# Layer 2 of a two-layer interaction network in fp32: seven half-width products over tile pairs instead of eight, with sums of products on GpSimd

## The chip, the cores and the metric

The kernel runs on one core of a Trainium2 chip. The metric is the device time of one execution in microseconds (us). A core has a matrix engine (TensorE, PE in the profile; its weight loads have a row of their own, PEld), VectorE (DVE), ScalarE (ACT), GpSimd (POOL) and SyncE (SP, which here only starts transfers). SBUF is the on-chip memory of 128 partitions, PSUM the accumulator memory that PE writes, in banks of 128 x 512 fp32 numbers; DVE and ACT read and write both.

## The reference

`x` has 4096 rows, 32 fields, 16 embedding positions; row and position together are 65,536 sites. All is fp32.

```python
def _batchnorm(h, gamma, beta):                       # over rows and positions
    mean = jnp.mean(h, axis=(0, 2), keepdims=True)
    var = jnp.var(h, axis=(0, 2), keepdims=True)
    return (h - mean) * jax.lax.rsqrt(var + EPS) * gamma[None, :, None] + beta[None, :, None]

def _cin_layer(out, x, W, b, gamma, beta):
    r, _, e = x.shape
    h = jnp.einsum('rne,rfe->rnfe', out, x).reshape(r, -1, e)
    h = jnp.einsum('rce,oc->roe', h, W) + b[None, :, None]
    return _batchnorm(h, gamma, beta)

h1 = _cin_layer(x, x, W1, b1, g1, beta1)              # 128 channels from 32 x 32 products
out, direct1 = (h1[:, :64], h1[:, 64:])
direct2 = _cin_layer(out, x, W2, b2, g2, beta2)       # 128 channels from 64 x 32 products
return jnp.concatenate([direct1, direct2], axis=1).sum(axis=-1)
```

## The kernel before

The sites lie along the free axis, in 128 tiles of 512. Tiles 2c and 2c+1 form one of 64 chunk pairs (the index `c` of the code; a pair below): one tile from each half of the sites.

**Layer 1** makes, for each tile, products of fields with fields (`z`, DVE, L208), multiplies them with the weights (PE, L218 and L220), and reads the sum out of PSUM (ACT, L176, L179, L189). DVE takes batch-norm statistics (L79) and sums over positions (L192). The 64 kept channels of a pair go to DRAM as `hs[c]`. Each tile has two loads, `a` and `b`, of 512 KB; each has three buffers, and SP issues them in the order of the tiles. The accumulators of four tiles are opened at once by four matmuls that use 32 rows of the array each (L218); `psum1` has eight banks.

**Between the layers** the batch-norm of layer 1 becomes a scale and a shift. Four small matmuls spread them to the partitions of layer 2, and a few matmuls without use (`running`) keep PE busy.

**Layer 2** has 2048 products per site, 16 blocks of 128: four groups `i` of 16 kept channels, and in each four chunks `k` of eight fields. For each tile and group ACT applies scale and shift to the group's channels into a PSUM tile (`factor`, L296), DVE multiplies it by four chunks of fields at once (`z`, 128 x 2048, L306), and PE accumulates four full-width matmuls (L311). A tile thus has 16 matmuls in one bank; ACT reads it out (L316), DVE takes statistics (L79) and position sums (L318). Per pair SP loads two `b` of 1024 KB and four `a` of 512 KB.

Each engine works strictly in the order in which it got its instructions. A product tile has three buffers (`zpool`), a factor tile three, an accumulator four banks. At the end the batch-norm of layer 2 is applied to the 128 x 2048 position sums of each half (L328), which are then stored.

Of the kernel before, what the change touches and what calls it, by code (L numbers as in the profile page):

```python
# [35 lines left out]
RT = T // EMB  # L36
KEEP = 64
EPS = 1e-5
WRAP = 48
GROUP = 8  # L40
SG = 16


@with_exitstack
def tile_cin(ctx: ExitStack, tc: tile.TileContext, xa, xb, xr, w1, w1m, w2, bn, out):
    nc = tc.nc

    const = ctx.enter_context(tc.tile_pool(name="const", bufs=1))
    dram = ctx.enter_context(tc.tile_pool(name="dram", bufs=1, space=bass.MemoryType.DRAM))
# [4 lines left out]
    bpool = ctx.enter_context(tc.tile_pool(name="bpool", bufs=3))  # L54
    apool = ctx.enter_context(tc.tile_pool(name="apool", bufs=8))
# [11 lines left out]
    class Stats:  # L67


        def __init__(self, n):  # L70
            self.n = n
            self.groups = const.tile([P, NT // SG, 3], FP, tag=f"groups{n}", name=f"groups{n}")
            nc.vector.memset(self.groups, 1.0)

        def add(self, t, h, bias=None):

            if t % SG == 0:
                self.stats = spool.tile([P, SG, 6], FP, tag="stats", name=f"stats{self.n}")
            nc.vector.bn_stats(self.stats[:, t % SG, :], h)  # L79
            if bias is not None:  # L80
                means = self.stats[:, t % SG, 1:5:3]
                nc.vector.tensor_scalar(means, means, bias, None, ALU.add)
            if t % SG == SG - 1:
                nc.vector.bn_aggr(self.groups[:, t // SG, 1:3], self.stats.rearrange("p a b -> p (a b)"))  # L84

        def scale_shift(self, gamma, beta):
# [13 lines left out]
            ss = const.tile([P, 3], FP, tag=f"ss{self.n}", name=f"ss{self.n}")  # L100
# [5 lines left out]

    select = const.tile([KEEP, 4, 16, 8], FP, tag="select", name="select")
    nc.gpsimd.memset(select, 1.0)  # L110
    nc.gpsimd.affine_select(
        out=select,
# [6 lines left out]
    )  # L119

    hs = [dram.tile([KEEP, 2 * T], FP, tag=f"h{c}", name=f"h{c}") for c in range(NC)]
    d1 = sums.tile([P, ROWS // 2], FP, tag="sum", name="d1")
    stats1 = Stats(1)

    with ExitStack() as one:
        wpool = one.enter_context(tc.tile_pool(name="wpool", bufs=1))
        lpool = one.enter_context(tc.tile_pool(name="lpool", bufs=3))
        rpool = one.enter_context(tc.tile_pool(name="rpool", bufs=1))
        psum = one.enter_context(tc.tile_pool(name="psum1", bufs=8, space=bass.MemoryType.PSUM))
# [7 lines left out]
        def load_main(t):  # L137
            a = lpool.tile([P, 2 * T], FP, tag="a", name="a")
            nc.sync.dma_start(  # L139
                a, bass.AP(xa.tensor, xa.offset + t * FIELDS * 2 * T, [[2 * T, FIELDS], [0, 4], [1, 2 * T]])  # L140
            )
            b = lpool.tile([P, 2 * T], FP, tag="b", name="b")
            nc.sync.dma_start(
                b,
                bass.AP(xb.tensor, xb.offset + (t * WRAP + 2) * T, [[T, FIELDS], [4 * T, 4], [1, 2 * T]]),
            )
            return a, b
# [6 lines left out]
        w2_sb = const.tile([P, 16, P], FP, tag="w2", name="w2_sb")  # L154
        nc.scalar.dma_start(w2_sb, w2)
        b1, g1, beta1, b2, g2, beta2 = (bn_sb[:, k : k + 1] for k in range(6))
        nc.vector.tensor_tensor(w1_sb, w1_sb, w1m_sb, ALU.add)  # L157

# [41 lines left out]
        for t in range(NT):  # L200
            s = t % GROUP
# [19 lines left out]
            if t > 0:  # L221
                finish(t - 1)
        last = finish(NT - 1)

    psum = ctx.enter_context(tc.tile_pool(name="psum2", bufs=4, space=bass.MemoryType.PSUM))
    factors = ctx.enter_context(tc.tile_pool(name="factors", bufs=3, space=bass.MemoryType.PSUM))
# [11 lines left out]
    low, high = slice(0, KEEP), slice(KEEP, P)  # L238


    keep_ps = psum.tile([P, 4, 2], FP, tag="ps", name="keep_ps")
    for i in range(4):
        nc.tensor.matmul(  # L243
            keep_ps[:, i, :],
            select[:, i].rearrange("k n f -> k (n f)"),
            ss1[low, 0:2],
            start=True,
            stop=True,
        )
# [21 lines left out]
    d2 = [sums.tile([P, ROWS // 2], FP, tag=f"sum{half}", name=f"d2_{half}") for half in range(2)]  # L271
    stats2 = Stats(2)

    def load_a(c, i):

        a = apool.tile([P, 2 * T], FP, tag="a", name="a")
        nc.sync.dma_start(a, hs[c][16 * i : 16 * (i + 1), :].unsqueeze(1).to_broadcast([16, 8, 2 * T]))
        return a

    def load_b(t):  # L280

        b = bpool.tile([P, 4, T], FP, tag="b", name="b")
        nc.sync.dma_start(b, bass.AP(xb.tensor, xb.offset + t * WRAP * T, [[0, 16], [4 * T, 8], [1, 4 * T]]))
        return b

    for c in range(NC):
        raw = []
        for half in range(2):
            t = 2 * c + half
            b = load_b(t)  # L290
            ps = psum.tile([P, T], FP, tag="ps", name="ps")
            for i in range(4):
                if half == 0:
                    raw.append(load_a(c, i))
                a = factors.tile([P, T], FP, tag="a", name="factor")
                nc.scalar.activation(  # L296
                    a,
                    raw[i][:, half * T : (half + 1) * T],
                    AF.Identity,
                    scale=keep[:, i, 0:1],  # L300
                    bias=keep[:, i, 1:2],
                )
                z = zpool.tile([P, 4, T], FP, tag="z", name="z")
                for js in ([slice(0, 1), slice(1, 4)] if t == 0 and i == 0 else [slice(0, 4)]):
                    n = js.stop - js.start
                    made = nc.vector.tensor_tensor(  # L306
                        z[:, js, :], a.unsqueeze(1).to_broadcast([P, n, T]), b[:, js, :], ALU.mult
                    )
                for k in range(4):
                    m = 4 * i + k  # L310
                    nc.tensor.matmul(ps, w2_sb[:, m, :], z[:, k, :], start=(m == 0), stop=(m == 15))  # L311
                if t == 0 and i == 1:
                    with tc.issue_after(made.ins):
                        write_direct()
            e = epool.tile([P, T], FP, tag="e", name="e")
            nc.scalar.activation(e, ps, AF.Identity, bias=b2)  # L316
            stats2.add(t, e)
            nc.vector.tensor_reduce(  # L318
                d2[half][:, c * RT : (c + 1) * RT],
                e.rearrange("p (r e) -> p r e", e=EMB),  # L320
                AX.X,
                ALU.add,
            )

    ss2, _ = stats2.scale_shift(g2, beta2)
    nc.vector.tensor_scalar(ss2[:, 2:3], ss2[:, 1:2], float(EMB), None, ALU.mult)
    for half in range(2):
        nc.vector.tensor_scalar(d2[half], d2[half], ss2[:, 0:1], ss2[:, 2:3], ALU.mult, ALU.add)  # L328
        nc.sync.dma_start(out[KEEP:, half * (ROWS // 2) : (half + 1) * (ROWS // 2)], d2[half])
# [54 lines left out]
```

## Time and profile before

| what | value |
|---|---|
| median of three runs (lowest to highest) | 2302.85 us (2297.73 to 2305.64) |
| the profiled execution's own time | 2299.39 us |
| its span in the profile | 2297.6 us |
| busy: PE, DVE, ACT, POOL | 98%, 76%, 32%, 0% |
| first matmul of layer 2 / last matmul's start | 525.5 us / 2283.9 us |
| DMA busy in layer 1 / layer 2 | above 90% / about 65% |

The profile covers one execution. Busy time is the time in which an engine had an instruction in work; a busy PE need not be at its peak, since its matmuls overlap. One fp32 matmul of the program is two records on PE, so layer 2's 2048 matmuls are 4096 records. Groups name the line, engine, operation, output and inputs, count, busy time and mean duration of one. A chain of waits follows the work that ended last back to what released it.

### The profile page before, as it was taken

What the parts mean: (1) busy time and instruction counts of PE and PEld (TensorE: products, weight loads), DVE (VectorE), ACT (ScalarE), POOL (GpSimd) and SP (SyncE); (2) the same over time, 40 slices, a digit from 0 to 9 for tenths busy, and PEclk for the clock granted to TensorE, in tenths of its full rate; (3) what the DMA queues carried; (4) which work ended last, traced back from release to release, by engine and by line L of the source; (5) the groups of instructions that cost most, each with busy time, mean ns of one, the idle gap of its engine ahead of it and who ended that gap; (6) DMA issues with size and microseconds to landing.
All of it is one profiled execution on the core that took longest, in us unless ns stands there. A gap on an engine that the chain in (4) does not pass through costs nothing.

```text
span 2297.6 us, 15702 instructions
## 1 busy us (share of the span) xinstructions
PE 2256.0 (98%) x5394; PEld 985.3 (43%) x5394; DVE 1743.5 (76%) x1147; ACT 739.1 (32%) x1028; POOL 1.8 (0%) x6
## 2 busy tenths in 40 slices
PE   7899999999999999999999999999999999999997
PEld 3334444444444444444444444444444444444443
DVE  7678888877777777777777777777777777777775
ACT  3345555553222222222222222222222222222221
POOL 0000000000000000000000000000000000000000
PEclk9999999999999999999999999999999999999999
DMA  9999999965666666666666666666666666666661
GB/s 353 309 359 343 333 332 338 328 239 151 155 156 147 155 151 157 153 158 155 151 147 155 156 146 155 151 155 158 154 158 148 146 156 155 146 154 154 153 140 39
DMA packets 100687, 433.84 MB, mean 189 GB/s; under 512 B 11776, under 2 KB 11776, under 8 KB 83712
## 3 DMA queue, kind: packets, MB, share of 16 engines
q1 hardware_dynamic: 94752, 413.18, 67.3%
q10 hardware_dynamic: 5856, 19.67, 2.3%
q8 instruction: 42, 0.69, 0.1%
q14 instruction: 37, 0.30, 0.1%
HBM read 412.88 MB, written 19.92 MB: 188 GB/s over the span
## 4 chain that ended last, share of the span: by engine, by line
PE 94%; DMA 4%; DVE 1%; issue 0%; SPq 0%; ACT 0%; DVEq 0%; ACTq 0%
PE ps L311 76%; PE ps L220 16%; DMA b<-in_xb 3%; PE ps L218 1%; DVE z L208 1%; DMA a<-in_xa 0%; PE running L232 0%; DVE stats L79 0%; DVE z L306 0%; SPq L139 0%; DVE groups L84 0%; DVE d L328 0%; DVEq L380 0%; PE keep_ps L243 0%; ACT factor L296 0%
## 5 line engine op out<-in xcount | busy, mean ns | idle before, releaser
L311 PE MATMUL ps<-z,w_sb 128*128 128x512 f32 x4096 | 1758.4, 592 | 0.5 <-DVE z L306 0.5
L306 DVE TENSOR_TENSOR z<-factor,b 128x2048 f32<-128x2048 f32 (+1 forms) x513 | 1171.6, 2284 | 436.6 <-PE ps L311 435.7
L311 PEld LDWEIGHTS ps<-z,w_sb 128*128 128x128 f32 x4096 | 778.1, 190 | 980.8 <-issue 975.3
L296 ACT ACTIVATE factor<-a,keep 128x512 f32<-128x512 f32 x512 | 399.9, 782 | 1225.0 <-DVE z L306 1112.7
L220 PE MATMUL ps<-z,w_sb 128*128 128x512 f32 x1024 | 457.2, 604 | 16.5 <-DVE z L208 16.5
L208 DVE TENSOR_TENSOR z<-a,b 128x2048 f32<-128x2048 f32 x128 | 293.1, 2290 | 84.3 <-PE ps L220 45.8
L220 PEld LDWEIGHTS ps<-z,w_sb 128*128 128x128 f32 x1024 | 193.8, 192 | 278.5 <-issue 245.8
L79 DVE BATCH_NORM_STATS2 stats<-e 128x6 f32<-128x512 f32 x255 | 174.7, 685 | 11.5 <-ACT e L316 8.8
L176 ACT ACTIVATE e<-ps,bn_sb 128x512 f32<-128x512 f32 x127 | 87.3, 687 | 262.2 <-PE ps L220 223.0
L316 ACT ACTIVATE e<-ps,bn_sb 128x512 f32<-128x512 f32 x128 | 87.9, 687 | 52.5 <-PE ps L311 52.5
L189 ACT ACTIVATE ed<-ps,bn_sb 64x512 f32<-64x512 f32 x128 | 87.4, 683 | 2.7 <-ACT sd L91 0.3
L179 ACT ACTIVATE kept<-ps,bn_sb 64x512 f32<-64x512 f32 x128 | 85.7, 670 | 2.2 <-DVE stats L79 2.2
L318 DVE TENSOR_REDUCE d<-e 128x32 f32<-128x512 f32 x128 | 85.7, 669 | 0.0
L218 PE MATMUL ps<-zr,w_sb 32*128 32x512 f32 x256 | 37.4, 655 | 8.1 <-DVE w_sb L157 8.1
L192 DVE TENSOR_REDUCE d<-ed 128x32 f32<-128x512 f32 x64 | 42.8, 669 | 0.6 <-ACT ed L189 0.6
L218 PEld LDWEIGHTS ps<-zr,w_sb 32*128 32x128 f32 x256 | 10.2, 186 | 31.6 <-issue 23.5
L205 DVE TENSOR_TENSOR zr<-r 128x512 f32<-128x512 f32 x16 | 10.9, 682 | 5.0 <-DMA r<-in_xr 5.0
L232 PE MATMUL running<-w_sb 128*128 128x512 f32 x10 | 6.3, 770 | 3.3 <-ACT ed L189 3.3
L84 DVE BATCH_NORM_AGGREGATE groups<-stats 128x2 f32<-128x96 f32 x16 | 9.3, 579 | 0.0
L232 PEld LDWEIGHTS running<-w_sb 128*128 128x128 f32 x10 | 2.0, 218 | 5.9 <-ACT ed L189 4.1
L251 DVE COPY keep<-keep_ps 128x8 f32<-128x8 f32 x1 | 0.2, 166 | 5.4 <-PE keep_ps L243 5.4
L328 DVE TENSOR_SCALAR d<-d,ss 128x2048 f32<-128x2048 f32 x2 | 2.6, 1344 | 0.0
(27 smaller groups left out, 14.1 us busy)
## 6 DMA issues: line engine op xcount, KB each, us to landing
b<-in_xb SPq DMA_DIRECT2D x128, 1024.0 KB, 7.2
a<-h SPq DMA_DIRECT2D x256, 512.0 KB, 6.9
b<-in_xb SPq DMA_DIRECT2D x128, 512.0 KB, 6.8
a<-in_xa SPq DMA_DIRECT2D x128, 512.0 KB, 6.2
h<-kept ACTq DMA_DIRECT2D x64, 256.0 KB, 5.8
r<-in_xr SPq DMA_DIRECT2D x16, 512.0 KB, 6.8
out<-d SPq DMA_DIRECT2D x2, 1024.0 KB, 4.5
w_sb<-in_w ACTq DMA_DIRECT2D x1, 1024.0 KB, 9.9
```

The source lines that it names most:

```text
L79: nc.vector.bn_stats(self.stats[:, t % SG, :], h)
L176: nc.scalar.activation(e, ps, AF.Identity, bias=b1)
L179: nc.scalar.activation(h[:, half * T : (half + 1) * T], ps[:KEEP, :], AF.Identity, bias=b1[:KEEP])
L189: nc.scalar.activation(ed, ps[KEEP:, :], AF.Identity, bias=b1[KEEP:])
L208: nc.vector.tensor_tensor(z, a.rearrange("p (a t) -> p a t", a=2).unsqueeze(2).to_broadcast([P, 2, 2, T]), b.rearrange("p (b t) -> p b t", ...
L218: nc.tensor.matmul(ps, w1_sb[rows, 4 + s // 4, :], zr[rows, :], start=True, stop=False)
L220: nc.tensor.matmul(pss[t], w1_sb[:, m, :], z[:, m // 2, m % 2, :], start=False, stop=(m == 3))
L296: nc.scalar.activation(a, raw[i][:, half * T : (half + 1) * T], AF.Identity, scale=keep[:, i, 0:1], bias=keep[:, i, 1:2],)
L306: made = nc.vector.tensor_tensor(z[:, js, :], a.unsqueeze(1).to_broadcast([P, n, T]), b[:, js, :], ALU.mult)
L311: nc.tensor.matmul(ps, w2_sb[:, m, :], z[:, k, :], start=(m == 0), stop=(m == 15))
L316: nc.scalar.activation(e, ps, AF.Identity, bias=b2)
L318: nc.vector.tensor_reduce(d2[half][:, c * RT : (c + 1) * RT], e.rearrange("p (r e) -> p r e", e=EMB), AX.X, ALU.add,)
```

## The change

Layer 2 handles both tiles of a pair together. In three of four groups (0, 1, 2) the product is taken as a 2 x 2 block product by the seven-product scheme of Strassen (in Winograd's form): the blocks of the weights are channel halves by chunk pairs, those of the data chunk pairs by the two tiles. Group 3 (`PLAIN`) keeps its eight products, in a form that adds to the same accumulators, and is computed first (`STAGES`); a group's work within a pair is called a stage below.

- A matmul has 64 output channels instead of 128. Accumulators are halves of four banks (`x62`, `x34`, `x57`, `x11`: the digits are the products in the lower and upper 64 partitions). Neighbouring matmuls write to opposite halves.
- Sums of weight blocks (`combine_weights`) are made once on DVE, in layer 1. A difference of field chunks of each pair's second tile (`difference`) is made on DVE in layer 1 for 16 pairs at a time and kept in DRAM; `load_bx` reads it.
- Three sums of products per stage (`strassen`; `t2`, `t1`, `t4`, 128 x 1024 each) are made on GpSimd.
- The accumulators of a pair are combined into the two tiles' results during the next pair (`combine`), in steps that stand between the products on DVE and ACT. One of the two operands of each sum lies in PSUM.
- `queue` fixes the order of DVE, ACT, PE and GpSimd in layer 2. PSUM has six accumulator banks and two factor banks over the whole kernel. `b` has two buffers, `a` six; the first pair's loads are issued in layer 1 (`EARLY`).
- The four small matmuls between the layers become one; at the end both position sums are scaled on two engines and stored in four parts.

```diff
+    psum = ctx.enter_context(tc.tile_pool(name="psum", bufs=6, space=bass.MemoryType.PSUM))
+    factors = ctx.enter_context(tc.tile_pool(name="factors", bufs=2, space=bass.MemoryType.PSUM))
...
+    def load_bx(c):
+        bx = bpool.tile([P, 4, T], FP, tag="bx", name="bx")
+        at = xb.offset + ((2 * c + 1) * WRAP + 2) * T
+        nc.sync.dma_start(bx[:, 0:2], bass.AP(xb.tensor, at, [[0, 16], [4 * T, 8], [1, 2 * T]]))
+        d = diffs[c // DIFF][c % DIFF * 8 : (c % DIFF + 1) * 8, :]
+        to = bx[:, 2:4].rearrange("p q t -> p (q t)")
+        nc.sync.dma_start(to, d.unsqueeze(0).to_broadcast([16, 8, 2 * T]))
+        return bx
+    EARLY = [(72, lambda: load_b(0)), (80, lambda: load_bx(0))]
+    EARLY += [(88 + 8 * k, lambda i=i: load_a(0, i)) for k, i in enumerate(STAGES)]
...
+        def difference(g):
+            xs = []
+            for j in (2, 0):
+                x = rpool.tile([P, 2 * T], FP, tag="r", name="x")
...
+                nc.sync.dma_start(x, bass.AP(xb.tensor, at, [[2 * WRAP * T, DIFF], [4 * T, 8], [1, 2 * T]]))
+                xs.append(x)
+            nc.vector.tensor_tensor(xs[0], xs[0], xs[1], ALU.subtract)
+            nc.scalar.dma_start(diffs[g], xs[0])
...
+            if t == 8:
+                combine_weights()
+            with tc.issue_after(loads[-1].ins):
+                if t % 16 == 12 and t // 16 < NC // DIFF:
+                    difference(t // 16)
+                for first, load in EARLY:
+                    if t == first:
+                        early.append(load())
...
+    def ordinary(sums_, z1, z2):
+        for k in range(4):
+            q = k % 2
+            a11, a21, a12, a22, s1, s2, s3, s4 = weights(PLAIN, q)
+            sums_.matmul(3, s4 if k < 2 else neg_sb[:, 0, q], z2[:, k])
+            sums_.matmul(2, a11 if k < 2 else a12, z1[:, k])
+            sums_.matmul(5, s1 if k < 2 else neg_sb[:, 1, q], z2[:, k])
+            sums_.matmul(4, a21 if k < 2 else a22, z1[:, k])
+    def strassen(sums_, i, z1, z2, stop):
+        t = tpool.tile([P, 3, 2, T], FP, tag="t", name="t")
+        b11, b21, b22, t3 = z1[:, 0:2], z1[:, 2:4], z2[:, 0:2], z2[:, 2:4]
+        t2, t1, t4 = (t[:, k] for k in range(3))
+        for to, x, y, op in ((t2, t3, b11, ALU.add), (t1, b22, t2, ALU.subtract), (t4, b21, t2, ALU.subtract)):
+            queue("pool", lambda: nc.gpsimd.tensor_tensor(to, x, y, op))
+        w = [weights(i, q) for q in range(2)]
+        sums_.matmul(1, w[0][0], b11[:, 0], stop)
+        sums_.matmul(0, w[1][0], b11[:, 1], stop)
+        for (x, kx, bx), (y, ky, by) in (
+            ((3, 7, b22), (2, 2, b21)),
+            ((6, 5, t2), (7, 6, t3)),
+            ((5, 4, t1), (4, 3, t4)),
+        ):
+            for q in range(2):
+                sums_.matmul(x, w[q][kx], bx[:, q], stop and q == 1)
+                sums_.matmul(y, w[q][ky], by[:, q], stop and q == 1)
+    def combine(c, sums_):
+        x62, x34, x57, x11 = sums_.banks
+        both = cpool.tile([P, T], FP, tag="both", name="both")
+        act(both[low], x11[high])
+        act(both[high], x11[low], bias=b2[low])
+        yield
+        add(both, both, x11)
+        yield
+        e = cpool.tile([P, 2, T], FP, tag="e", name="e")
+        add(e[:, 0], both, x62)
+        yield
+        u2 = cpool.tile([P, T], FP, tag="u2", name="u2")
+        act(u2[low], e[low, 0], bias=b2[low])
+        act(u2[high], e[low, 0], bias=b2_swapped[low])
+        yield
+        u3 = cpool.tile([P, T], FP, tag="u3", name="u3")
+        add(u3, u2, x57)
+        yield
+        u3_low = cpool.tile([KEEP, T], FP, tag="u3l", name="u3_low")
+        act(u3_low, u3[high])
+        yield
+        add(e[:, 1], u3, x34)
+        add(e[low, 0], u3_low, x57[low])
+        yield
+        dve(lambda: stats_x.add(c, e[:, 0]))
+        dve(lambda: stats_y.add(c, e[:, 1]))
+        yield
+        dve(
+            lambda: nc.vector.tensor_reduce(
+                d2[:, :, c, :], e.rearrange("p s (r e) -> p s r e", e=EMB), AX.X, ALU.add
+            )
+        )
+        yield
...
+    nc.scalar.activation(dy, dy, AF.Identity, scale=ss2[:, 0:1], bias=ss2[:, 2:3])
+    nc.vector.tensor_scalar(dx, dx, swapped[:, 0:1], swapped[:, 2:3], ALU.mult, ALU.add)
```

The order of DVE in layer 2 before, for one tile (`e` is the tile read out of PSUM, `d2` its position sums):

```order
L306 TENSOR_TENSOR z_4768<-factor_4766,b_4763 128x2048
L306 TENSOR_TENSOR z_4776<-factor_4774,b_4763 128x2048
L306 TENSOR_TENSOR z_4784<-factor_4782,b_4763 128x2048
L79 BN_STATS stats2_4158<-e_4759 128x6
L318 TENSOR_REDUCE d2_0_2720<-e_4759 128x32
L306 TENSOR_TENSOR z_4792<-factor_4790,b_4763 128x2048
```

and now, from the first product of a pair to the second product of its third stage (`z` and `z2` are the products of the pair's two tiles; `both`, `e`, `u3` belong to the pair before):

```order
L390 TENSOR_TENSOR z_5110<-f_5108,b_5091 128x2048
L390 TENSOR_TENSOR z2_5114<-f_5112,bx_5093 128x2048
L386 TENSOR_TENSOR both_5118<-both_5118,x11_4968 128x512
L390 TENSOR_TENSOR z_5138<-f_5116,b_5091 128x2048
L386 TENSOR_TENSOR e_5140<-both_5118,x62_4965 128x512
L390 TENSOR_TENSOR z2_5147<-f_5142,bx_5093 128x2048
L386 TENSOR_TENSOR u3_5149<-u2_5144,x57_4967 128x512
L390 TENSOR_TENSOR z_5173<-f_5151,b_5091 128x2048
L386 TENSOR_TENSOR e_5140<-u3_5149,x34_4966 128x512
L386 TENSOR_TENSOR e_5140<-u3_low_5153,x57_4967 64x512
L390 TENSOR_TENSOR z2_5179<-f_5177,bx_5093 128x2048
```

Behind these stand two BN_STATS, the two products of the last stage and one TENSOR_REDUCE of 128x2x32. The number of products is the same, eight per pair; five sums have come between them.

PE in a stage of seven products (`t` are GpSimd's sums; before, all of layer 2 stood here as 2048 like rows, `L311 MATMUL ps<-z,w_sb 128x512`). Each of the last three kinds of row pairs comes twice, once for each chunk:

```order
L416 MATMUL x11_6616<-z_6682,w2_sb_181 64x512 x2
L416 MATMUL x34_6614<-z2_6688,s_sb_182 64x512
L416 MATMUL x62_6613<-z_6682,w2_sb_181 64x512
...
L416 MATMUL x62_6613<-t_6694,s_sb_182 64x512
L416 MATMUL x57_6615<-z2_6688,s_sb_182 64x512
...
L416 MATMUL x57_6615<-t_6694,s_sb_182 64x512
L416 MATMUL x34_6614<-t_6694,w2_sb_181 64x512
```

A stage has 14 matmuls of half width, of which six read the product tiles alone, four need `t2` or stand beside one that does, and the last four need `t1` and `t4`.

More of the change, by code (lines that the diff above doesn't have):

```diff
@@ L268, in write_direct @@
             )
[L271 to L284, printed above, removed]
@@ L286, in tile_cin @@
-    for c in range(NC):
[L287 to L323, printed above, removed]
@@ new lines, in tile_cin @@
+    nc.vector.tensor_copy(swapped[high], ss2[low])
+    dx, dy = (d2[:, s].rearrange("p c r -> p (c r)") for s in range(2))
+    nc.scalar.activation(dy, dy, AF.Identity, scale=ss2[:, 0:1], bias=ss2[:, 2:3])
+    nc.vector.tensor_scalar(dx, dx, swapped[:, 0:1], swapped[:, 2:3], ALU.mult, ALU.add)
+    first, second = slice(0, ROWS // 2), slice(ROWS // 2, ROWS)
+    for engine, d, half, m, rows in (
+        (nc.sync, dx, low, 1, second),
+        (nc.sync, dx, high, 0, first),
+        (nc.scalar, dy, low, 0, second),
+        (nc.scalar, dy, high, 1, first),
+    ):
+        engine.dma_start(out[KEEP + m * KEEP : KEEP + (m + 1) * KEEP, rows], d[half])
```

186 lines of the change are left out of this document (152 added, 34 removed).

## The prediction

> **What bounds the kernel now.** I read first the busy time by stretches (columns: busy time and instruction count of each engine, granted clock, DMA share, GB/s), then the groups of instructions, then the chain of waits in order of time.
>
> ```profile
> 20.00:100.00 80.00, 75.50 (x196) 30.86 (x195) 58.41 (x48) 38.19 (x60) 0.00 (x0) 0.98 1.01 331
> 100.00:200.00 100.00, 91.49 (x232) 37.51 (x234) 80.17 (x66) 44.61 (x70) 0.00 (x0) 0.97 0.98 349
> 200.00:300.00 100.00, 100.00 (x269) 42.12 (x270) 87.88 (x72) 52.21 (x81) 0.00 (x0) 1.00 0.94 332
> 300.00:400.00 100.00, 100.00 (x270) 41.97 (x269) 87.24 (x74) 50.76 (x80) 0.00 (x0) 1.00 0.94 336
> 400.00:480.00 80.00, 80.00 (x213) 33.74 (x212) 70.19 (x57) 42.23 (x66) 0.00 (x0) 1.00 0.93 327
> 480.00:520.00 40.00, 36.75 (x96) 15.46 (x95) 28.52 (x33) 19.19 (x31) 0.00 (x0) 0.99 0.57 187
> 1000.00:2000.00 1000.00, 1000.00 (x2331) 442.72 (x2331) 748.73 (x442) 277.74 (x365) 0.00 (x0) 1.00 0.66 154
> ```
>
> Layer 1 is held by DMA (0.98 to 1.01) at least up to 100 us and by PE from 200 us on, with DMA still at 0.94. Layer 2 (the last row) has PE busy without a gap at full clock; DVE has a quarter free, POOL nothing to do. The chain says the same: one unbroken piece of PE.
>
> ```profile
> 527.21 1757.29 PE ps L311 x4094
> ```
>
> 4094 records in 1757.29 us are 0.429 us each, so a full-width matmul (two records) takes 0.858 us, and a pair of tiles (32 matmuls) 27.46 us. Only fewer PE passes or a shorter start or tail can help; every other engine must then fit into the new period.
>
> **PE.** A seven-product stage has 14 half-width matmuls, the ordinary one 16, so a pair has 3 x 14 + 16 = 58. If two matmuls on opposite column halves run at once, these are 29 full ones: 24.88 us, 2.58 us less, **-164.8 us** over 64 pairs. That the halves overlap is the first open cost; no row shows it. The nearest are layer 1's matmuls on 32 of the array's rows, four of them side by side (the timeline's start and length, then the line's min/median/max in ns):
>
> ```profile
> 304.87 1.14 PE L218 MATMUL ps<-zr,w_sb 32*128 32x512 f32 x8
> 305.94 0.30 PEld L220 LDWEIGHTS ps<-z,w_sb 128*128 128x128 f32 x2 [0.76 <-issue]
> L218 PE MATMUL ps<-zr,w_sb x256: 587/692/1215, 8.1 to 500.4; 32*128 32x512 f32 x128
> L311 PE MATMUL ps<-z,w_sb x4096: 592/592/697, 525.5 to 2283.9; 128*128 128x512 f32 x196
> ```
>
> Eight records take 1.07 us from start to next start; in a row they would take 3.43 us. So tiles of the array do overlap, and the two passes of each (0.858 us) account for all but 0.21 us. A record's length is 587 or 692, and the full-width line has the same 697 as its longest: about 0.105 us on entering a tiling and as much on leaving. Layer 2 enters its tiling once, so I take 0.858 us for a pair of half matmuls. The upper ends are 1.07 us (the toll is paid by each pair) and 1.716 us (no overlap: columns, unlike rows, need two data streams over all 128 partitions).
>
> [...]
>
> **DVE, ACT and POOL per pair.**
>
> ```profile
> L306 DVE TENSOR_TENSOR z<-factor,b 128x2048 f32<-128x2048 f32 x511 | 1169.3, 2289 | 435.7 <-PE ps L311 435.7
> L205 DVE TENSOR_TENSOR zr<-r 128x512 f32<-128x512 f32 x16 | 10.9, 682 | 5.0 <-DMA r<-in_xr 5.0
> L79 DVE BATCH_NORM_STATS2 stats<-e 128x6 f32<-128x512 f32 x255 | 174.7, 685 | 11.5 <-ACT e L316 8.8 <-ACT e L176 2.7
> L318 DVE TENSOR_REDUCE d<-e 128x32 f32<-128x512 f32 x128 | 85.7, 669 | 0.0
> L296 ACT ACTIVATE factor<-a,keep 128x512 f32<-128x512 f32 x512 | 399.9, 782 | 1225.0 <-DVE z L306 1112.7 <-DMA b<-in_xb 106.5 <-DVE keep L251 5.8
> L179 ACT ACTIVATE kept<-ps,bn_sb 64x512 f32<-64x512 f32 x128 | 85.7, 670 | 2.2 <-DVE stats L79 2.2
> 1009.96 0.68 DVE L79 BATCH_NORM_STATS2 stats<-e 128x6 f32<-128x512 f32 x1
> 1010.55 0.67 DVE L318 TENSOR_REDUCE d<-e 128x32 f32<-128x512 f32 x1
> L111 POOL TENSOR_SCALAR_AFFINE_SELECT select<-select 64x512 f32<-64x512 f32 x1 | 1.1, 1083 | 0.1
> L110 POOL MEMSET select<- 64x512 f32 x1 | 0.5, 518 | 0.3 <-POOLq L371 0.3
> ```
>
> DVE: 8 products x 2.289, 5 sums x 0.685, 2 statistics x 0.685 and one reduction of 1024 columns (0.669 plus 512 x 1.04 ns, the slope from 682 to 2289, = 1.20): 18.31 + 3.43 + 1.37 + 1.20 = 24.3 us, against 21.0 before. Followers start 0.09 us before an end (0.68 long, next start after 0.59), so 16 instructions occupy about 22.9 us. DVE fits, with 2 us to spare instead of over 6. ACT: 8 x 0.782 + 5 x 0.67 = 9.6 us.
>
> POOL has nine sums of 128 x 1024, the second open cost. Below: 1.04 us (a memset writes 512 columns in 0.518). Above: 3.1 us (two reads and a write, each at that rate). Nearest is the affine select, which reads and writes: 1.083 for 512, so 2.17 us; I take **2.2 us**, 19.8 us per pair. [...]
>
> More than the sum, the loop counts. DVE's `both` waits for ACT, and ACT for the first matmuls of the last stage, which stand in PE's queue behind the last four of the third stage, which need the sixth POOL sum. From one `both` to the next: DVE `both`, product, `e`, product 0.69 + 2.20 + 0.60 + 2.20; six POOL sums; on PE two pairs 1.72, the next pair 0.86 and its drain 0.16 (592 less 429 ns); two ACT reads 1.3; hand-overs of 0.06 to 0.1, about 0.4. That is 10.1 us plus six sums: 23.3 us at 2.2, under PE's 24.88. It passes PE at 2.46 us per sum. What queues behind `both` is every later product, so a late loop stops PE a stage later. With margins of 1.6 (loop) and 2.0 us (DVE) I add 0.15 us per pair for hand-overs that miss each other, **+10 us** (from 0 to 77, which is 1.2 us a pair).
>
> **DMA and layer 1.**
>
> ```profile
> b<-in_xb SPq DMA_DIRECT2D x128, 1024.0 KB, 7.2
> a<-h SPq DMA_DIRECT2D x256, 512.0 KB, 6.9
> r<-in_xr SPq DMA_DIRECT2D x16, 512.0 KB, 6.8
> L176 ACT ACTIVATE e<-ps,bn_sb 128x512 f32<-128x512 f32 x127 | 87.3, 687 | 262.2 <-PE ps L220 223.0 <-DVE stats L79 18.5 <-DMA a<-h 10.5
> ```
>
> In layer 2 a pair loads 4096 KB before and after (one `b` of 1024, two halves of `bx` of 512, four `a`); the share rises from 0.66 to 0.73, and buffers come free about a pair (25 us) ahead of a landing time of 7 us, so it costs nothing; without that cover each stage would wait up to 7 us. In layer 1 come eight loads and four stores of 512 KB for `difference` and 4 MB of early loads, about 10.5 MB; at 332 GB/s 32 us of transfers, put into SP's one queue ahead of the next tiles. Idle DMA time from 100 to 480 us is about 20 us (shares 0.98, 0.94, 0.94, 0.93). The first two differences (tiles 12 and 28) fall where DMA sets the pace: 1.5 MB each, 9 us. The next `r` load uses a difference's buffer and waits on SP for its store, so I take **+12 us**, from 0 to 32. DVE's weight sums (four of 0.69 and two small ones) and differences (1.2 each) lie in its waits. Six PSUM banks instead of eight cost nothing: the bank that is reopened first at a set of four was left three tiles (over 10 us) earlier, and its reads take 0.69 + 0.67 + 0.68 us after the matmul; uncovered, 2 us for every four tiles would be 64 us.
>
> **Start and tail.**
>
> ```profile
> L306 DVE TENSOR_TENSOR z<-factor,b 128x512 f32<-128x512 f32 x1 | 0.7, 691 | 0.8 <-ACT factor L296 0.8
> 2284.58 0.69 ACT L316 ACTIVATE e<-ps,bn_sb 128x512 f32<-128x512 f32 x1 [13.11 <-PE ps L311]
> 2289.07 2.60 DVE L328 TENSOR_SCALAR d<-d,ss 128x2048 f32<-128x2048 f32 x2
> L263 ACT ACTIVATE d<-d,direct 128x2048 f32<-128x2048 f32 x1 | 2.1, 2094 | 0.0
> ```
>
> The first matmul waited for a product of 512 columns (0.69); now the ordinary stage needs both full products, 2 x 2.29: **+4 us**. After the last matmul come three sums instead of one read (+1.4), a second statistics and a longer reduction (+1.1), one more aggregate and five small copies (+1.4), and 2.09 us on ACT instead of 1.34 for the first half (+0.75): **+5 us**.
>
> **Sum.** 2299.39 (own time; span 2297.6) - 164.8 + 10 + 12 + 4 + 5 = 2165.6. The median of the runs shown is 3.5 above that execution: **2169 us**.
>
> **The rivals.**
>
> A. *POOL becomes the bound.* Past 2.46 us per sum the loop is 10.1 + 6 x sum. At 2.65 it gives 26.0 us, 2230 in all. With start, tail and layer 1 costing 21 us, layer 2 must stay under 27.13 us per pair, so from **2.84 us** per sum the change loses: at 3.1 us 28.7 us a pair, 1837 + 21 against 1757, 2404 us. For it: two inputs, and no row with two. Against: the select is at 2.17. 0.10 for 2.46 to 2.84, 0.07 above.
>
> B. *Each pair of half matmuls pays the toll*: 1.07 us, 31.0 us per pair, 64 x 3.57 + 21 = +250, 2552 us. For: 1.07 is what the row shows. Against: 697 appears on full-width matmuls only as a maximum, so the toll goes with the switch. 0.05.
>
> C. *The halves do not overlap* (the change doesn't do what it says): 58 x 0.858 = 49.8 us, 3750 us. 0.05.
>
> D. *POOL and DVE shut each other out of SBUF*: 24.3 + 19.8 = 44.1 us per pair, 3390 us. No row has POOL at work beside DVE. [...] 0.03.
>
> **How the numbers follow.** The forecast (PE sets layer 2) has 0.70 and its own range is 2140 to 2205. A below 2.84 us reaches 2300, so 2135 to 2290 holds about 0.8. A measurement here tells about 0.3% from no change. Faster: 0.70 + 0.08 = 0.78; within 0.3%: 0.02 (A near 2.84); slower: 0.07 + 0.05 + 0.05 + 0.03 = 0.20.
>
> **What would show it.** Right: half-width matmuls whose starts come in twos with 0.43 us between passes; PE at 58 per 24.9 to 25.1 us with no wait for GpSimd over some tenths of a us; GpSimd sums spaced 2.2 to 2.4 us; first layer-2 matmul near 541 us. A: long PE waits for `t`, GpSimd without gaps. B and C: PE busy all the time at over 25 us per pair while DVE waits for it. D: DVE's products longer than 2.29 us. A first layer-2 matmul after 562 or before 529 us would make the layer-1 term wrong.

## The result, and the profile after

The changed kernel takes **2176.78 us** (median of four runs, 2174.55 to 2179.46) against 2300.48 us beside it: ratio 0.946, 95% interval 0.9438 to 0.9482. The profiled execution took 2176.87 us, with a span of 2175.2 us. The forecast was 2169 us, in a range of 2135 to 2290.

The page of the changed kernel, the busy times of section 1 and groups of section 5:

```profile
PE 2104.6 (97%) x8716; PEld 736.2 (34%) x8716; DVE 1909.9 (88%) x1422; ACT 854.4 (39%) x1221; POOL 1355.8 (62%) x582
...
L432 POOL TENSOR_TENSOR t<-z,z 128x1024 f32<-128x1024 f32 x192 | 456.8, 2379 | 779.7 <-DVE z L390 779.7
L432 POOL TENSOR_TENSOR t<-z,t 128x1024 f32<-128x1024 f32 x384 | 903.1, 2374 | 15.1
...
L390 DVE TENSOR_TENSOR z<-f,bx 128x2048 f32<-128x2048 f32 x256 | 582.7, 2276 | 0.0
```

DVE is busy for 88% of the span, GpSimd for 62%. The view of the matmuls' line (min/median/max in ns, first and last start):

```profile
L416 PE MATMUL x<-z,w_sb x2560: 592/592/1114, 538.7 to 2149.2; 128*64 128x512 f32 x197
...
L416 PE MATMUL x<-t,w_sb x768: 592/592/644, 552.8 to 2152.6; 128*64 128x512 f32 x192
```

Layer 2 runs from the first matmul at 538.7 us to the last start at 2152.6: 1613.9 us instead of 1758.4. A sum on GpSimd takes 2.38 us, a product on DVE 2.28 us as before. The timeline of PE in the middle of layer 2:

```profile
999.91 0.59 PE L416 MATMUL x<-z,w_sb 128*64 128x512 f32 x1
999.92 0.59 PE L416 MATMUL x<-z,neg_sb 128*64 128x512 f32 x1
1000.34 0.59 PE L416 MATMUL x<-z,w_sb 128*64 128x512 f32 x1
1000.35 0.59 PE L416 MATMUL x<-z,neg_sb 128*64 128x512 f32 x1
```

Two half-width matmuls start within 0.01 us, the next two 0.43 us later. Each matmul has two passes, so two matmuls side by side take 0.86 us. The two halves of the array's columns work at once and cost no toll.

The chain of waits, in order of time, over one turn of its loop (start, length, what):

```profile
1019.68 21.69 PE x L416 x99
1041.36 0.02 issue
1041.39 0.59 ACT both L383
...
1041.99 0.69 ACT both L383
...
1042.71 0.04 DVE both L386
...
1046.11 2.29 DVE z L390
...
1048.53 2.38 POOL t L432
...
1062.77 2.40 POOL t L432
...
1069.94 0.04 issue
1069.98 1.07 PE x L416 x3
```

The turn from 1019.68 to 1069.98 is 50.30 us, for two pairs. PE alone would need 2 x 24.88 = 49.76. In the turn PE has 21.69 us, ACT's copies for `both` and the hand-over 1.34, DVE 5.8 (1042.71 to 1048.53), and nine sums without a gap 21.4 (1048.53 to 1069.94). `both` holds back the products behind it on DVE, these feed the pair's nine sums, and the sums feed the matmuls whose results the next `both` but one waits for. So this loop, with GpSimd in it, sets the pace in place of PE, by 0.27 us a pair.

Where the 122.4 us between the two spans come from:

| part | before | after | measured | forecast |
|---|---|---|---|---|
| to the first matmul of layer 2 | 525.5 | 538.7 | +13.2 | +16 (layer 1 +12, start +4) |
| layer 2, first to last matmul start | 1758.4 | 1613.9 | -144.5 | -154.8 |
| last matmul start to the end | 13.7 | 22.6 | +8.9 | +5 |

Between the layers, the rows of PE's timeline ahead of its first matmul of layer 2, before and after:

```profile
518.21 4.29 PE L232 MATMUL running<-w_sb 128*128 128x512 f32 x6 [3.25 <-ACT ed L189]
522.42 1.25 PE L243 MATMUL keep_ps<-ss,select 64*128 64x2 f32 x8
```

```profile
528.80 3.60 PE L325 MATMUL running<-w_sb 128*128 128x512 f32 x8
532.70 0.35 PE L341 MATMUL keep_ps<-blocks,spread 64*128 64x8 f32 x2 [0.30 <-DVE blocks L334]
```

Before, the matmuls without use (`running`) wait 3.25 us for ACT and then stand in front of the small matmuls of the scale and shift (`keep_ps`). Now they are done before DVE has made those ready.

### The profile page after: what moved, and what is told of

It is laid out like the page before. It is cut to its first block, busy times and chain, and to the rows that moved or that the text cites. A ratio compares the mean times of both kernels' runs of the same rounds, so it can differ in the third digit from the quotient of the medians.

```text
span 2175.2 us, 23541 instructions
## 1 busy us (share of the span) xinstructions
PE 2104.6 (97%) x8716; PEld 736.2 (34%) x8716; DVE 1909.9 (88%) x1422; ACT 854.4 (39%) x1221; POOL 1355.8 (62%) x582
## 4 chain that ended last, share of the span: by engine, by line
PE 42%; POOL 27%; DVE 10%; issue 9%; DMA 8%; ACT 2%; SPq 1%; DVEq 0%; POOLq 0%; ACTq 0%
PE x L416 32%; POOL t L432 27%; PE ps L307 9%; DMA b<-in_xb 5%; DVE z L390 4%; DVE z L295 4%; ACT both L383 2%; DMA x<-in_xb 1%; DMA r<-in_xr 1%; DVE stats L97 1%; PE ps L305 1%; DMA a<-in_xa 0%; DVE e L386 0%; DMA h<-kept 0%; SPq L200 0%
## 5 line engine op out<-in xcount | busy, mean ns | idle before, releaser
L416 PE MATMUL x<-z,w_sb 128*64 128x512 f32 x2560 | 1076.3, 594 | 0.0
L416 PE MATMUL x<-z,s_sb 128*64 128x512 f32 x2048 | 954.7, 594 | 4.5 <-DVE z L390 4.5
L432 POOL TENSOR_TENSOR t<-z,z 128x1024 f32<-128x1024 f32 x192 | 456.8, 2379 | 779.7 <-DVE z L390 779.7
L432 POOL TENSOR_TENSOR t<-z,t 128x1024 f32<-128x1024 f32 x384 | 903.1, 2374 | 15.1
L416 PE MATMUL x<-t,s_sb 128*64 128x512 f32 x1536 | 698.4, 594 | 0.0
L383 ACT ACTIVATE f<-a,keep 128x512 f32<-128x512 f32 x512 | 398.3, 778 | 637.9 <-DVE z L390 635.1
L390 DVE TENSOR_TENSOR z<-f,b 128x2048 f32<-128x2048 f32 x256 | 582.5, 2275 | 0.9 <-ACT f L383 0.8
L390 DVE TENSOR_TENSOR z<-f,bx 128x2048 f32<-128x2048 f32 x256 | 582.7, 2276 | 0.0
L307 PE MATMUL ps<-z,w_sb 128*128 128x512 f32 x1024 | 461.5, 608 | 26.5 <-DVE z L295 26.1
L307 PEld LDWEIGHTS ps<-z,w_sb 128*128 128x128 f32 x1024 | 195.0, 194 | 291.5 <-issue 234.3
```

What stands on the lines that cost most here:

```text
L307: nc.tensor.matmul(pss[t], w1_sb[:, m, :], z[:, m // 2, m % 2, :], start=False, stop=(m == 3))
L383: return queue("act", lambda: nc.scalar.activation(to, source, AF.Identity, **scale_bias))
L390: dve(lambda: nc.vector.tensor_tensor(z, a.unsqueeze(1).to_broadcast([P, 4, T]), b, ALU.mult))
L416: queue("pe", lambda: nc.tensor.matmul(self.of[x], w, b, start=start, stop=stop))
L432: queue("pool", lambda: nc.gpsimd.tensor_tensor(to, x, y, op))
```

## The experiments

In the kernels with an unchanged layer 1 the first matmul of layer 2 comes anywhere from 538.5 to 546.0 us. So parts are compared by the traces, and totals only where the difference is larger than that. "Layer 2" is always the time from its first to its last matmul start.

### A late `both`

```diff
             if k in (1, 2, 3):
                 step()
+            if k == 1:
+                step(2)
...
-            if k == 0:
-                step(2)
```

This puts `both` behind the first product of the second stage on DVE; nothing is left out.

> The first sum of the combination (both) is issued one product later on DVE, behind the first product of the second stage instead of in front of it. Theory (loop): of the 25.15 us per pair that layer 2 takes now, 0.27 us over the 24.88 of the matrix engine come from the loop both - two products - six GpSimd sums - last matmuls of the third stage - first matmuls of the fourth - two ScalarE reads - both; issuing both later takes a product (2.2 us) out of the loop, so PE is bound at 24.88 to 24.92 us per pair and the whole is about 2160 us (-17). Rival (the 0.27 us belong to the half-width matmuls themselves, a toll on PE): still 25.1 to 25.2 us per pair, 2175 to 2179 us.

Measured: 2165.05 us (ratio 0.9419, 0.9403 to 0.9435). The stretch from 1000 to 2000 us (PE, PEld, DVE, ACT, POOL: busy time and count; clock, DMA share, GB/s) of the changed kernel, then of this one:

```profile
1000.00:2000.00 1000.00, 994.51 (x4614) 328.20 (x4612) 914.79 (x641) 371.90 (x516) 844.22 (x360) 1.00 0.71 168
```

```profile
1000.00:2000.00 1000.00, 1000.00 (x4662) 334.74 (x4660) 928.85 (x649) 377.36 (x523) 851.14 (x362) 1.00 0.70 169
```

Its matmul line:

```profile
L416 PE MATMUL x<-z,w_sb x2560: 592/592/1116, 546.0 to 2140.4; 128*64 128x512 f32 x197
L416 PE MATMUL x<-t,w_sb x768: 592/592/643, 559.3 to 2143.8; 128*64 128x512 f32 x192
```

PE has no gap left and does 1% more work in the same time (4662 records instead of 4614). Layer 2 takes 1597.8 us, 16.1 less, where 17 were expected; the median gains only 12, since layer 1 varies: in the profiled execution (2168.03 us) layer 2 began 7.3 us later than in that of the changed kernel. The loop through `both` was real, and a better place for one DVE instruction takes it away.

### Sums of half the size, and a fourth sum

The first kernel forms each sum over one chunk instead of two (`to[:, 0]`, `x[:, 0]`, `y[:, 0]`); the second chunk's sums are left out and its matmuls read the first's. The second kernel adds an unread sum in front of the three of each stage.

> GpSimd's sums are made for the first of the two chunks only (128 x 512 instead of 128 x 1024), and the matmuls of both chunks read that one: the second chunk's sums are left out, all else stays. Theory (loop): sums of about 1.25 us leave the loop at 10.1 + 6 x 1.25 = 17.6 us, PE never waits for them, 24.88 us per pair, 2160 us, as in the run with the later sum. Rival (PE's own toll): 25.1 to 25.2 us per pair, 2175 to 2179. The length of a sum also splits its price: if it is proportional to columns, 1.18 us; with a fixed part of 0.15 us, 1.26 us.

> A fourth sum of the same size, which nobody reads, stands in front of the three of each seven-product stage. Theory (loop): two stages now hold 8 sums of 2.37 us, 10.1 + 19.0 = 29.1 us per pair against 27.46 before the change: about 2420 us, slower than the kernel before. It checks the point of rival A, 27.13 us per pair. Counting GpSimd's work alone (12 x 2.37 = 28.4 us) gives about 2385 us. If GpSimd were off the path, about 2177.

A group of the kernel with half sums, then one of the kernel with four sums and its matmul line:

```profile
L432 POOL TENSOR_TENSOR t<-z,t 128x512 f32<-128x512 f32 x384 | 482.5, 1278 | 15.0
```

```profile
L432 POOL TENSOR_TENSOR spare<-z,z 128x1024 f32<-128x1024 f32 x192 | 454.5, 2367 | 584.0 <-DVE z L390 584.0
```

```profile
L416 PE MATMUL x<-z,w_sb x2560: 592/592/1112, 538.5 to 2394.3; 128*64 128x512 f32 x197
L416 PE MATMUL x<-t,w_sb x768: 592/592/1080, 552.6 to 2401.1; 128*64 128x512 f32 x192
```

Half sums: 2163.88 us, layer 2 1594.1 us, 24.9 a pair. Four sums: 2424.96 us, layer 2 1862.6 us, 29.1 a pair, close to what twelve sums of 2.37 us alone would take (28.4): GpSimd is busy for 968.6 of the 1000 us from 1000 to 2000. So nine sums a pair (21.4 us) fit behind PE's 24.88 and twelve do not; a third more GpSimd work turns the gain of 123 us into a loss of 128. The 29.1 us expected came from a loop that closes in one pair; the chain of the changed kernel shows another, so that the number was met is luck. From the two lengths a sum costs 2.14 ns a column and 0.18 us.

### Factors in SBUF

One word changes: the pool `factors` lies in SBUF instead of PSUM, so that DVE's products in layer 2 read both operands from SBUF.

> The factor tiles lie in SBUF instead of PSUM, so each product on DVE has two SBUF inputs; nothing else changes. If DVE and GpSimd then shut each other out for whole instructions: 8 products (18.2 us) and 9 sums (21.3 us) cannot overlap, at least 39.5 us per pair, at most 45.6: 3095 to 3485 us, with products or sums that read longer than 2.28 and 2.37 us. If they do not: 2177 us within 5, with the same lengths.

Measured: 2982.52 us, less than the least that was expected for engines that shut each other out (3095). Its groups, the last from layer 1, where GpSimd stands still; then a product of layer 2 (start, length):

```profile
L432 POOL TENSOR_TENSOR t<-z,t 128x1024 f32<-128x1024 f32 x384 | 1507.8, 3946 | 15.1
L390 DVE TENSOR_TENSOR z<-f,b 128x2048 f32<-128x2048 f32 x256 | 942.9, 3683 | 0.9 <-ACT f L383 0.9
L295 DVE TENSOR_TENSOR z<-a,b 128x2048 f32<-128x2048 f32 x128 | 291.8, 2282 | 47.6 <-DMA b<-in_xb 32.5
```

```profile
1018.51 4.43 DVE L390 TENSOR_TENSOR z<-f,b 128x2048 f32<-128x2048 f32 x1
```

Each kind grows by 1.3 to 1.6 us, and a pair takes 37.8 us. Two operands in SBUF alone do not slow a product: layer 1's have them too and take 2.28 us. Beside GpSimd's sums the product shown takes 4.43 us, nearly a product and a sum together (4.66). If products and sums took strict turns, 8 x 2.28 + 9 x 2.375 = 39.6 us would follow; all but 1.8 of it does. In the changed kernel, beside the same sums and with its factor in PSUM, a product takes 2.28 us; here, with the factor in SBUF, it takes 3.7. Rival D was a real danger; the factors in PSUM are what kept it out.

### Halves in twos

The order of the matmuls within a block becomes lower, lower, upper, upper instead of lower, upper, lower, upper.

> In the seven-product stages the matmuls go to the column halves two and two (lower, lower, upper, upper) instead of alternating; 36 of the 58 matmuls of a pair stand in such groups of four. Theory 1 (matmuls start in order, and each starts as soon as its half is free): the second lower one runs beside the first upper one, four still take 1.72 us apart from the ends, at most 0.5 us per pair more, 2177 to 2210 us. Theory 2 (only direct neighbours on opposite halves overlap, and no pass of a later one fills in): each group of four takes 2.57 us, 9 groups x 0.86 = 7.7 us per pair more, about 2670 us. No overlap at all in a group: 3.43 us, 15.4 us more, about 3165 us.

Measured: 2175.22 us, layer 2 from 539.1 to 2151.4 (1612.3 us instead of 1613.9), unchanged. From 1000 to 2000 us PE does 4619 records in 996.5 us of work: two passes side by side every 0.43 us, as in the changed kernel (4614 in 994.5). So neighbours in the queue need not alternate one by one: the groups of four cost nothing here.

### Layer 1: no difference, the difference on GpSimd, and the kernel before with its loads held

The first kernel leaves the differences of layer 1 out (layer 2 reads plain fields in their place). The second takes and stores them on GpSimd:

```diff
-        rpool = one.enter_context(tc.tile_pool(name="rpool", bufs=2))
+        rpool = one.enter_context(tc.tile_pool(name="rpool", bufs=1))
+        xpool = one.enter_context(tc.tile_pool(name="xpool", bufs=2))
...
-            nc.vector.tensor_tensor(xs[0], xs[0], xs[1], ALU.subtract)
-            nc.scalar.dma_start(diffs[g], xs[0])
+            nc.gpsimd.tensor_tensor(xs[0], xs[0], xs[1], ALU.subtract)
+            nc.gpsimd.dma_start(diffs[g], xs[0])
```

> The differences of field chunks are left out of layer 1 (their eight loads, four sums and four stores); layer 2 reads plain fields in their place, with the same number of bytes. The first matmul of layer 2 stood at 538.7 us, against 525.5 before the change. Theory (the differences cost layer 1 most of its 14 us): it comes at 526 to 531 us, the whole at 2165 to 2170 us. Rival (the 4 MB of early loads cost it): 535 to 539 us.

> The differences are made by GpSimd (idle in layer 1) and stored through its own queue, with two buffers of their own; bytes are unchanged. Theory (waits in order: DVE stood 32.8 us before the four sums, ScalarE 29.3 us behind their stores, and DVE 20.6 us for loads that wait for a difference's buffer): most of what the run without differences gains comes back, first matmul of layer 2 at 529 to 533 us, the whole 2167 to 2172 us. Rival (the 6 MB of transfers themselves set the loss): within 2 us of 538.7, the whole unchanged.

Measured: 2142.93 us without differences, 2147.26 us with them on GpSimd (ratio 0.934, 0.9325 to 0.9356). The first matmul of layer 2 comes at 504.7 and 508.4 us instead of 538.7. The second number rules out the bytes and fits the theory of waits that stand in order: the same bytes move, and all but 3.7 of the 34 us that the differences cost are gone. But both numbers lie below the 525.5 us of the kernel *before*, which no theory had foretold. That called for a third kernel: the one before the change, with nothing but its layer-2 loads held behind the last load of layer 1.

```diff
-            b = load_b(t)
+            with tc.issue_after(loads[-1].ins):
+                b = load_b(t)
...
-                    raw.append(load_a(c, i))
+                    with tc.issue_after(loads[-1].ins):
+                        raw.append(load_a(c, i))
```

> The kernel before the change, with the loads of layer 2 held behind the last load of layer 1 on SP's queue (in the kernel before, the first of them stand among layer 1's loads from 45 us on, since their buffers are free). If these early loads are what keeps layer 1 of the kernel before on DMA until 200 us, its layer 1 becomes PE-bound from 20 us on as in the run without differences, the first layer-2 matmul comes at 504 to 508 us instead of 525.5, and the time is about 2300 - 19 = 2281 us. If they are hidden anyway, the first layer-2 matmul stays at 523 to 527 us and the time at 2300 us.

SP's rows of the kernel before, with two loads of layer 2 (L283, L277) among those of layer 1:

```profile
44.20 0.59 SPq L143 DMA_DIRECT2D b<-in_xb  x1
44.85 0.59 SPq L283 DMA_DIRECT2D b<-in_xb  x1
...
47.65 0.79 SPq L143 DMA_DIRECT2D b<-in_xb  x1
48.48 0.74 SPq L277 DMA_DIRECT2D a<-h  x1
```

A stretch of layer 1 after the change, then two of the kernel before with its loads held:

```profile
100.00:200.00 100.00, 89.47 (x227) 37.42 (x226) 75.84 (x64) 44.58 (x69) 0.00 (x0) 0.95 0.92 315
```

```profile
20.00:100.00 80.00, 80.00 (x213) 33.77 (x212) 70.04 (x57) 41.97 (x65) 0.00 (x0) 1.00 0.95 340
100.00:200.00 100.00, 100.00 (x270) 41.95 (x269) 87.62 (x73) 51.16 (x80) 0.00 (x0) 1.00 0.94 334
```

The layer-2 matmuls of that kernel:

```profile
L315 PE MATMUL ps<-z,w_sb x4096: 592/592/697, 504.6 to 2262.9; 128*128 128x512 f32 x196
```

Measured: 2278.23 us (ratio 0.9905, 0.9889 to 0.9921), first matmul of layer 2 at 504.6 us. With the loads held PE has no gap from 20 to 200 us. So the kernel before lost 21 us to loads that came long before they were needed. The change holds them back too (`EARLY` begins at tile 72, the rest follow the last load of layer 1). Without its differences it reaches layer 2 at 504.7 us, as this kernel does at 504.6; the differences then cost 34 us. After the change DVE stands at the differences and at late `r` loads, and ACT behind the stores of the differences (who waits for whom up to 530 us: total us, times, longest):

```profile
DVE x L243 <- DMA x<-in_xb: 32.8, 4, 8.9
...
ACT e L263 <- DVE x L243: 29.3, 4, 8.4
DVE zr L292 <- DMA r<-in_xr: 20.6, 6, 5.4
```

A DVE that waits up to 8.9 us for a difference's loads holds back every later product and statistic. The GpSimd kernel takes away this wait, the shared buffers and the store on ACT's queue together; which of the three weighs most was not separated.

### The last stores

Three kernels look at the 12.4 us between the first store and the end (7.2 us before the change): the order of the two stores on ACT swapped; the two stores of `dy` made one from 128 partitions; all four stores on SP's queue. The last two start from the combined version, told in the next section.

> The last two of the four output stores change places, so that the two queues store different halves of the partitions at a time instead of the same half. From the first store's issue to the end the changed kernel takes 12.4 us, the kernel before 7.2 us for the same bytes (164 to 254 GB/s against 393 to 418). Theory (a store from 64 partitions runs at half the rate, and two from the same half share it): about 8 to 9 us, the end 3.5 to 4.5 us earlier. Rival (four stores cost more than two whatever their partitions): 12.4 us.

> The combined version, with one more edit: the two stores of dy, each from 64 partitions, become one from all 128. In the changed kernel the four 64-partition stores keep the DMA engines busy without a gap for about 10 us at 202 to 240 GB/s; the kernel before stored the same 2.1 MB from 128 partitions at 400 GB/s and more in half that time. If the number of partitions in a store sets its rate, dy's 1.05 MB goes at 400 instead of 210 GB/s: 2.6 us instead of 5, the span's end comes 2.4 us sooner behind the last instruction of DVE (14.1 us in the changed kernel to 11.7), and the time is 2131 - 2.4 = 2128.7 us. If it is the two queues, or the sum of what is stored, the rate stays at 210 GB/s and the end where it was: 2131 us.

> The combined version with all four last stores on SP's queue (two of them were on ACT's). The kernel before had its two stores on SP's queue alone and moved 400 GB/s and more; with two queues at once the DMA engines are just as busy but move 202 to 240 GB/s. If the two queues hinder each other, one queue stores the 2.1 MB in about 5 us instead of 10, and the time is 2131 - 4 = 2127 us. If a store from 64 partitions is slow in itself, the rate stays at about 210 GB/s, and the time at 2131 us, or up to 1 us more since SP issues four in a row.

The stores after the change, in stretches (the last three columns: clock, DMA share, GB/s):

```profile
2164.00:2166.00 2.00, 0.00 (x0) 0.00 (x0) 0.00 (x0) 0.00 (x0) 0.00 (x0) 0.50 1.08 225
2166.00:2168.00 2.00, 0.00 (x0) 0.00 (x0) 0.00 (x0) 0.00 (x0) 0.00 (x0) 0.50 1.03 213
```

The same in the kernel before, in the one with the wide store, and in the one with one queue:

```profile
2292.00:2294.00 2.00, 0.00 (x0) 0.00 (x0) 0.00 (x0) 0.00 (x0) 0.00 (x0) 0.50 1.02 418
```

```profile
2130.00:2140.00 10.00, 0.00 (x0) 0.00 (x0) 0.00 (x0) 0.00 (x0) 0.00 (x0) 0.50 0.13 53
```

```profile
2116.00:2118.00 2.00, 0.00 (x0) 0.00 (x0) 0.00 (x0) 0.00 (x0) 0.00 (x0) 0.50 1.03 242
2118.00:2120.00 2.00, 0.00 (x0) 0.00 (x0) 0.00 (x0) 0.00 (x0) 0.00 (x0) 0.50 0.96 274
2120.00:2122.00 2.00, 0.00 (x0) 0.00 (x0) 0.00 (x0) 0.00 (x0) 0.00 (x0) 0.50 1.06 320
```

*Swapped order:* from the first store to the end 11.9 us instead of 12.4, where 3.5 to 4.5 less were expected. Missed. *Wide store:* 2145.23 us, 14 us slower than the combined version. Missed, with a reason that can be read: the DMA share is 0.13, the work of about two engines of sixteen, at 53 GB/s. The store's outermost dimension had only two entries; that this is the cause was not shown, since no run varied it alone. *One queue:* first store to end 11.35 us against 12.7 in the combined version; the rate climbs from 242 to 320 GB/s, where the combined version moves 197 to 254. That is 1.4 us of the expected 4.

What is shown is that the four stores from 64 partitions go at about half the rate with all DMA engines busy (213 to 229 GB/s against 393 to 418), and that neither the pairing of the halves (197 to 262 GB/s in the swapped order) nor the choice of queue (242 to 320) brings the full rate back. That the number of partitions is the cause is not shown by itself: the one store from 128 was the one with two entries outermost, at 53 GB/s. A store from 128 partitions that also has many rows outermost needs another layout of `d2`, and was not tried.

### The three edits together

The late `both`, the difference on GpSimd, and five more `running` matmuls (`keep_running(7)` for `keep_running(2)`) between the layers.

> Three edits of the changed kernel together: the late `both` (step(2) moved behind z1 at k == 1), the difference taken and stored by GpSimd out of buffers of its own, and seven `running` matmuls instead of two behind keep_ps, so that PE is not idle for 4.5 us before layer 2. The first two act in different places (the loop of layer 2: 17 us; the waits that stand in order on DVE and SP in layer 1: 30 us), so if both mechanisms are as the earlier runs say, they add: 2177 - 17 - 30 = 2130 us. The seven matmuls should take away the half clock of layer 2's first 6 us: 3 us more, 2127 us, with the first 14 layer-2 matmuls 0.43 us a record apart instead of 0.86. Rival: both gains were the same slack in part (a layer 1 that ends earlier only moves a wait), and the sum stays at 2140 or above.

Measured: **2131.11 us** (ratio 0.9265, 0.9252 to 0.9279). First matmul of layer 2 at 509.4 us, layer 2 1598.4 us: the two large gains add, as expected. The seven matmuls took away the half clock at the start and brought nothing of the 3 us expected. The start of layer 2 after the change, then in this kernel:

```profile
538.65 1.11 PE L416 MATMUL x<-z,s_sb 128*64 128x512 f32 x1 [4.54 <-DVE z L390]
539.56 1.06 PE L416 MATMUL x<-z,s_sb 128*64 128x512 f32 x1
```

```profile
509.39 0.64 PE L417 MATMUL x<-z,s_sb 128*64 128x512 f32 x1 [0.25 <-DVE z L391]
509.87 0.59 PE L417 MATMUL x<-z,s_sb 128*64 128x512 f32 x1
```

The half clock after 4.54 us of idle PE is gone (0.43 us a pass instead of 0.86 for the first 6 us, where the granted clock was 0.50), yet layer 2 is as long as with the late `both` alone (1597.8).

With all four stores on SP's queue as well the kernel takes **2128.17 us** (ratio 0.926, 0.9244 to 0.9276), 49 us less than the change. By their intervals it and the combined version are alike; the trace gives the 1.4 us told above. Its layer 2 takes 1597.8 us too. The first 30 us of layer 2 with the late `both` alone, then in this kernel:

```profile
546.00:576.00 30.00, 28.30 (x118) 8.83 (x120) 28.87 (x17) 12.38 (x15) 21.47 (x10) 0.93 0.63 156
```

```profile
505.60:535.60 30.00, 27.09 (x118) 8.96 (x120) 28.88 (x17) 12.36 (x15) 21.47 (x10) 1.00 0.64 156
```

At full clock PE has done the same 118 records after 30 us as with 6 us at half clock; it has only waited more. DVE and GpSimd have done the same work in both, and they set the pace of the first stages. In the combined version the longest records of PE in layer 2 take 1.06 us, as long as those at half clock after the change; with one queue the longest take 0.64. Layer 2 is 0.6 us longer in the combined version.

## Why the prediction was right, point by point

- **PE, -164.8 us: right.** The halves overlap fully: two half matmuls take 0.86 us without a toll, the lowest of the three prices. Rivals B and C are out by the timeline, and layer 2 without the loop runs at 24.9 us a pair; with the loop it takes 25.2, just above the 24.9 to 25.1 that the prediction named.
- **GpSimd's sum, 2.2 us: 2.38.** The estimate from the affine select was 8% low. Rival A's loss is out at this size, but less clearly than 0.17 suggested: the loop did pass PE a little, and a fourth sum per stage makes the kernel slower than before.
- **The loop and the +10 us: the mechanism right, its shape not, the term mis-sized.** By the prediction's own loop, 10.1 + 6 x 2.375 = 24.4 us stays under PE's 24.88, and PE would not wait. The loop that the chain shows closes over two pairs, with nine sums and 21.69 us of PE in it, and passes PE by 0.54 us per two pairs. Layer 2 is 21.6 us over 64 x 24.88. The late `both` takes away 16.1 of it; the 5.5 that stay include the first stages, in which PE waits for DVE and GpSimd. So the loop alone cost 16 us, not 10.
- **Layer 1, +12 us: the size right (+14.0 to the last matmul of layer 1, which ended at 528.97 instead of 514.96 us), the reason wrong.** The prediction counted the early loads as a cost of the change; they were already there before, at a worse time, and moving them gained 21 us. The price of the differences was put at their bytes, 12 us and at most 32 with the early loads. It was 34 us, of which all but 3.7 are waits and not bytes: DVE stands at a difference whose loads have not landed, ACT behind its store, and `r` loads wait for its buffers. Only the last of these waits was in the prediction. Two errors of opposite sign met in one term, so that its size came out is luck.
- **Start, +4 us: -0.8.** From the last matmul of layer 1 to the first of layer 2 it is 9.7 us instead of 10.5. The two full products cost what was counted: from ACT's first factor to the first matmul it is 5.4 us instead of 1.6. But the factor starts 4.3 us after the end of layer 1's last matmul instead of 9.0. The rows below the table show why: the matmuls without use no longer stand in front of the small ones. That weighs more than one small matmul in place of four (0.35 us instead of 1.25), and the prediction did not count it.
- **Tail, +5 us: +8.9.** The instructions cost less than counted (10.2 us from the last matmul start to the first store instead of 6.5, so +3.7 where +5 was counted), but the four stores from 64 partitions take 12.4 us instead of 7.2. The prediction had no term for them: it counted what DVE and ACT do and passed over the transfer that ends the kernel.
- **Rival D: rightly low.** The 0.03 was the author's estimate: no row of the kernel before has GpSimd beside DVE. Products stay at 2.28 us with the factor in PSUM. The kernel with factors in SBUF shows what D feared: with both operands of the products there, they take 3.68 us and the sums 3.95.

Against its own execution the sum was 11.3 us short (2165.6 for 2176.87): layer 2 took 10.3 more, the end 3.9 more, and the time to layer 2's first matmul 2.8 less than its terms. Sign and range needed only the first term and the bound on GpSimd.

## What to carry to other kernels

When engines pass work in a ring, look for loops that close over more than one round, and put a waiting instruction behind work that is ready: one DVE instruction moved by one product was worth 16 us here. Before a change is priced against a stretch of the kernel, ask whether that stretch is at its best: 21 of the 123 us gained came from loads that the old kernel issued far too early, so against that kernel with its loads held the change gains 101 us. Price the transfers that end a kernel by rows of like transfers, with the same partitions and the same outermost dimension, and not by their bytes alone.

## What was not expected of the hardware

- A two-input sum of 128 x 1024 on GpSimd took 2.38 us, one of 128 x 512 1.28 us. In layer 1 the difference took 2.34 us on GpSimd and 1.23 us on DVE.
- Stores from 64 partitions moved 213 to 229 GB/s at a DMA share of 0.91 to 1.08, against 393 to 418 GB/s from 128 at 0.94 to 1.02; a store with an outermost dimension of two moved 53 GB/s at a share of 0.13.
- After 4.54 us without work PE ran 6 us of layer 2 at half clock (granted clock 0.50, 0.86 us a pass). With the late `both` it cost nothing: after 30 us PE had done the same 118 records as at full clock, because other engines set the pace there.
